# Four kinds of TensorE transposes replaced by DMAs in a four-layer graph kernel, sums by columns of ones, and pairs of graphs taking turns by a fixed row of steps

## The chip, the cores and the metric

The kernel runs on one core of a Trainium2 chip. The metric is the device time of one execution in microseconds (us), as the median of several executions. A single core has no neighbour to compare with, so an execution counts as slow only when it lies over 1.5% above the fastest of the same kernel.

## The reference, cut to what matters

64 graphs of 256 nodes with 256 features pass through four attention layers, each followed by a layer norm. Three places matter here: the softmax of layer 0 (its division by the sums), the broadcast sum `s1 + s2` of layer 2, and the adjacency matrix, which every layer uses as a mask.

```python
# layer 0: 4 heads of 64
attn = jnp.einsum('bhnd,bhmd->bhnm', q, k) * scale
attn = jax.nn.softmax(jnp.where(adj[:, None] == 0, NEG, attn), axis=-1)
out = jnp.einsum('bhnm,bhmd->bhnd', attn, v).transpose(...).reshape(Bx, Nx, C) @ Wo.T + bo
x = _layernorm(x + layer_norm(out) * gamma + beta)
# layer 1: 8 heads of 32, then y @ W1 -> gelu -> @ W2 + b2
...
# layer 2
Wh = h @ W;  s1 = Wh @ a1;  s2 = Wh @ a2
e = leaky_relu(s1[:, :, None] + s2[:, None, :], 0.2)
h_prime = softmax(where(adj > 0, e, NEG_INF), axis=2) @ Wh
# layer 3: scores (hidden * a0) @ hidden.T, leaky_relu, mask, softmax, @ hidden
```

## The kernel before

The kernel works on 32 pairs of graphs. A pair is a Python generator; each `yield` ends one step. Several pairs are under way at once, and the order in which their generators are advanced is, for the most part, the order in which the instructions stand in the engines' queues. Before, a new pair starts every 15 steps, and `rest` puts empty steps in.

The parts that the change touches (cuts marked with `...`; `matmul` and `transpose` are helpers, so nearly all TensorE instructions carry one of two line numbers, L567 and L570 before, L561 and L564 after):

```python
PACE = 15
REST = {"xn": 1, "e3": 2, "products 4": 1, "wh": 2, "mask": 2, "products 2": 1, "xT2": 1}
...
    def products(i, cs, v, es, hd, oT, sums, gamma=None):
        m = P // hd
        for n, c in enumerate(cs):
            po = ps_m.tile([P, 2, N], F32, name="pm")
            ...                                        # the products into po[:, 0, :]
            for kc in range(QB):                       # layer 0: sums, one row per head
                for h in range(m):
                    z = (2 * h + kc) * 32
                    matmul(po[z:z + 32, 1, :], pick[:, c, :], es[n][:, h, kc * N:(kc + 1) * N], start=True, stop=True)
            nc.scalar.copy(oT[:, c, :], po[:, 0, :])
            if c == 0:
                nc.scalar.copy(sums, po[:, 1, :])
            else:
                nc.vector.tensor_tensor(sums, sums, po[:, 1, :], ALU.add)
...
        def behind(i, oT, zs):                         # layer 0, after the products
            pz = sums_of(zs)                           # TensorE transposes of the sums
            r = r_0[:, g * G + i]
            nc.vector.tensor_reduce(r..., pz..., AX.X, ALU.add)
            nc.vector.reciprocal(r, r)
            rr = att.tile([P, QB, D], F32, name="rr")
            nc.vector.tensor_copy(rr..., r...to_broadcast([P, QB * 4, 64]))
            yield
            pr = ps_m.tile([P, NC, N], F32, name="pm")
            for c in range(NC):
                for q in range(QB):
                    transpose(pr[:, c, q * P:(q + 1) * P], rr[:, q, c * P:(c + 1) * P], ident)
            nc.vector.tensor_tensor(oT, oT, pr, ALU.mult)
            yield
            ...                                        # product with Wo ("WoT" in the traces)
...
        # layer 2: exp(s1) along every partition ("the row")
        ex = small.tile([P, TB, 3], F32, name="ex")
        nc.scalar.activation(ex, wh[:, :, D:D + 3], AF.Exp)
        pt = ps_m.tile([P, G, N], F32, name="pm")
        for t in range(TB):
            transpose(pt[:, t // QB, t % QB * P:(t % QB + 1) * P], ex[:, t, 0:1].to_broadcast([P, P]), ident)
        e = act.tile([P, G, QB, N], F32, name="qT")
        for t in range(TB):
            i, kc = divmod(t, QB)
            nc.vector.tensor_scalar(e[:, i, kc, :], pt[:, i, :], ex[:, t, 1:2], ex[:, t, 2:3], ALU.mult, ALU.max)
        nc.vector.tensor_tensor(e, e, mask, ALU.mult)  # views left out
...
        # at the start of a pair: the edges the other way round
        for t in range(TB):
            i, q = divmod(t, QB)
            for kc in range(QB):
                transpose(pt[:, i, kc, q * P:(q + 1) * P], adjb[:, t, kc * P:(kc + 1) * P], identb)
```

## Time and profile before

| | before |
|---|---|
| time | 2787.66 us (2786.94 to 2789.51) |
| TensorE busy | 2679.1 of 2784.8 us (96%) |
| VectorE, ScalarE, GpSimd busy | 69%, 47%, 21% |
| one pair of graphs | 83.77 us |
| TensorE idle per 84 us in the middle | 0.86 us |

A busy share near 100% says which engine sets the pace, but not what a microsecond taken from it is worth. For that one needs the repeated stretch: with 0.86 us idle in 84, every microsecond of TensorE's stream that goes away shortens a pair by as much, as long as no new wait takes its place, and every microsecond of a new wait lengthens it by as much. The prediction shows the lines.

### The profile page before, as it was taken

Reading aid. Unit: us, or ns where it says so; the run is one execution under the profiler, and the core shown is the slowest. Engines: PE = TensorE matmul, PEld = TensorE weight load, DVE = VectorE, ACT = ScalarE, POOL = GpSimd, SP = SyncE. Lnnn points to the kernel's source line nnn. Section 1 sums busy time; section 2 is a strip of 40 time slices with the busy share of each in tenths; the row PEclk is TensorE's granted clock in tenths of the full one; section 3 lists DMA queues with packets and bytes.
Section 4 is the critical chain, followed back from the end, with each engine's and each line's share of the span. In section 5 each row is a group of like instructions: output and inputs, shape, how many; then the busy total and the mean of one; then the engine's idle time right before and its main releaser. Section 6 shows DMA issues by size and latency. Waiting matters only on the chain.

```text
span 2784.8 us, 45617 instructions
## 1 busy us (share of the span) xinstructions
PE 2679.1 (96%) x17288; PEld 1842.6 (66%) x17288; DVE 1931.9 (69%) x6346; ACT 1295.8 (47%) x1953; POOL 578.4 (21%) x1138
## 2 busy tenths in 40 slices
PE   4899999999999999999999999999999999999996
PEld 2566666666667666667676667676666676666664
DVE  3666767776767776767776767777767777667764
ACT  2445445445444445444445444445444445444441
POOL 1112212212212212212212222212222212122211
PEclk9899999999999999999999999999999999999998
DMA  3000000000000000000000000000000000000000
GB/s 110 24 9 23 24 16 18 22 16 24 24 16 16 23 16 24 18 21 16 24 16 24 16 24 16 24 16 24 16 24 16 24 16 24 8 16 9 9 8 16
DMA packets 57905, 57.78 MB, mean 21 GB/s; under 512 B 5073, under 2 KB 57297, under 8 KB 57681
## 3 DMA queue, kind: packets, MB, share of 16 engines
q1 hardware_dynamic: 50784, 50.34, 5.9%
q10 hardware_dynamic: 6896, 4.47, 0.6%
q8 instruction: 139, 2.28, 0.3%
q14 instruction: 86, 0.70, 0.1%
HBM read 38.02 MB, written 16.78 MB: 20 GB/s over the span
## 4 chain that ended last, share of the span: by engine, by line
PE 68%; DVE 20%; POOL 8%; issue 2%; ACT 1%; DMA 1%; ACTq 0%; POOLq 0%; DVEq 0%
PE pm L567 53%; PE ps L567 9%; PE pm L570 6%; POOL rstd L590 6%; DVE xn L598 4%; DVE e L643 3%; DVE st L583 3%; POOL ve L586 2%; DVE z L598 1%; DVE mv L584 1%; DVE e L637 1%; ACT e L635 1%; DVE y L796 1%; DVE xb L802 1%; DVE xb L598 1%
## 5 line engine op out<-in xcount | busy, mean ns | idle before, releaser
L635 ACT ACTIVATE e<-ps 128x1024 f32<-128x1024 f32 x384 | 372.4, 1022 | 356.4 <-PE ps L567 353.3
L567 PE MATMUL pm<-L_gnn_W,hT 128*128 128x256 f32 x2048 | 463.2, 379 | 0.0
L567 PE MATMUL pm<-xT,L_gnn_W 128*128 128x512 f32 x1024 | 450.8, 593 | 0.0
L567 PEld LDWEIGHTS pm<-L_gnn_W,hT 128*128 128x128 f32 x2048 | 383.9, 190 | 63.2 <-issue 15.1
L643 DVE SCALAR_TENSOR_TENSOR e<-e,mask 128x256 f32<-128x256 f32 x1024 | 399.2, 453 | 29.2 <-ACT e L635 29.2
L840 ACT ACTIVATE hT<-pm,b 128x512 f32<-128x512 f32 x256 | 176.0, 688 | 477.8 <-PE pm L567 477.8
L586 POOL TENSOR_SCALAR ve<-mv 128x2 f32<-128x2 f32 x384 | 93.8, 244 | 1328.1 <-DVE mv L584 1131.9
L567 PEld LDWEIGHTS pm<-xT,L_gnn_W 128*128 128x128 f32 x1024 | 192.7, 191 | 216.6 <-issue 214.2
L590 POOL TENSOR_TENSOR rstd<-ve,mhalf 128x2 f32<-128x2 f32 (+1 forms) x384 | 298.4, 777 | 26.7
L583 DVE BATCH_NORM_STATS2 st<-y 128x6 f32<-128x256 f32 x768 | 299.8, 408 | 5.6
L598 DVE TENSOR_SCALAR xn<-y,mv,rstd 128x256 f32<-128x256 f32 x384 | 163.2, 471 | 127.6 <-POOL rstd L590 127.6
L923 DVE TENSOR_TENSOR qT<-qT,kT 128x1024 f32<-128x1024 f32 x32 | 39.2, 1225 | 195.2 <-ACT kT L922 195.2
L637 DVE TENSOR_TENSOR e<-e,mask 128x1024 f32<-128x1024 f32 x128 | 148.0, 1218 | 12.4 <-ACT e L635 12.4
L567 PE MATMUL pm<-e,z 128*32 128x256 f32 x2048 | 149.3, 385 | 3.5 <-DVE e L643 2.8
L567 PE MATMUL pm<-e,v 128*32 128x256 f32 x2048 | 135.5, 382 | 15.8 <-DVE e L637 15.8
L567 PE MATMUL ps<-xT 32*128 32x256 f32 x2048 | 148.0, 403 | 0.0
L826 POOL TENSOR_TENSOR both<-y,xb 128x512 f32<-128x512 f32 x64 | 81.7, 1276 | 313.2 <-DVE y L825 313.2
L764 POOL TENSOR_TENSOR x<-x,beta 128x1024 f32<-128x1024 f32 x32 | 75.7, 2365 | 324.7 <-PE pm L570 324.7
L616 ACT ACTIVATE xT<-pm,beta,gamma 128x512 f32<-128x512 f32 x128 | 92.9, 774 | 103.9 <-PE pm L570 103.6
L567 PE MATMUL ps<-qT,kT 64*128 64x256 f32 x1024 | 127.9, 389 | 0.6 <-ACT e L635 0.6
L567 PE MATMUL pm<-v,qT 128*128 128x260 f32 x512 | 120.3, 389 | 3.3 <-DVE qT L899 3.3
L567 PEld LDWEIGHTS ps<-xT 32*128 32x128 f32 x2048 | 93.3, 185 | 45.4 <-issue 42.1
(144 smaller groups left out, 4347.7 us busy)
## 6 DMA issues: line engine op xcount, KB each, us to landing
x<-in_x SPq DMA_DIRECT2D x32, 512.0 KB, 3.8
adj<-in_adj SPq DMA_DIRECT2D x32, 512.0 KB, 3.8
out<-xn SPq DMA_DIRECT2D x32, 512.0 KB, 2.9
L_gnn_W<-in_L_gnn_W ACTq DMA_DIRECT2D x2, 1024.0 KB, 7.3
L_gnn_WqT<-in_L_gnn_WqT ACTq DMA_DIRECT2D x1, 256.0 KB, 4.8
L_gnn_WkT<-in_L_gnn_WkT ACTq DMA_DIRECT2D x1, 256.0 KB, 6.7
L_gnn_WvT<-in_L_gnn_WvT ACTq DMA_DIRECT2D x1, 256.0 KB, 7.7
L_gnn_WoT<-in_L_gnn_WoT ACTq DMA_DIRECT2D x1, 256.0 KB, 8.9
```

The lines of the kernel that those rows point to most:

```text
L567: in_order(nc.tensor.matmul(*args, **kw))
L570: in_order(nc.tensor.transpose(*args))
L583: nc.vector.bn_stats(st[:, q, :], src[:, t, 0:D])
L586: nc.gpsimd.tensor_scalar(ve[:, 0], mv[:, :, 1], EPS, None, ALU.add)
L590: nc.gpsimd.tensor_tensor(rstd, ve, mhalf[:, 0:k * QB].rearrange("p (k t) -> p k t", k=k), ALU.pow)
L598: nc.vector.tensor_scalar(dst[:, t, 0:D], src[:, t, 0:D], mv[:, q, 0:1], rstd[:, q:q + 1], ALU.subtract, ALU.mult)
L616: nc.scalar.activation(dst[:, c, :], pt, AF.Identity, bias=bias[:, c:c + 1], scale=scale[:, c:c + 1])
L635: nc.scalar.activation(e, ps, AF.Exp, scale=scale)
L637: nc.vector.tensor_tensor(e, e, mask.unsqueeze(1).to_broadcast([P, 2, QB * N]), ALU.mult)
L643: nc.vector.scalar_tensor_tensor(e[:, h, k], e[:, h, k], 1.0, mask[:, k], ALU.mult, ALU.mult, accum_out=sums[:, kc, c, j:j + 1])
L826: nc.gpsimd.tensor_tensor(both[:, i * QB:(i + 1) * QB, 0:D], o, xi, ALU.add)
L840: nc.scalar.activation(hT[:, f, :], pm, AF.Gelu, bias=b1[:, f:f + 1])
```

## The change

The intent is to free TensorE of transposes. The edges are transposed by DMA. Layer 0's sums are taken by columns of ones, 32 equal rows a head; their reciprocals go to device memory and come back repeated over 64 partitions. Layer 2's row goes out element by element and comes back repeated over all partitions. The empty steps and the fixed pace give way to one row of digits, each the age of the pair that takes the next step.

```diff
-PACE = 15
-REST = {"xn": 1, "e3": 2, "products 4": 1, "wh": 2, "mask": 2, "products 2": 1, "xT2": 1}
+ORDER = "001122333421243112124212133210321220100201010"
...
+        pz = ps_m.tile([P, N], F32, name="pm")
+        for kc in range(QB):
+            for h in range(4):
+                matmul(pz[32 * h:32 * h + 32, :], ones[:, 0:32], es[h // 2][:, h % 2, kc * N:(kc + 1) * N], ...)
+        nc.scalar.copy(oT, po)
+        nc.vector.reciprocal(sums, pz)
+        nc.scalar.activation(pz, sums, AF.Copy, accum_out=tally[i])
...
-            pz = sums_of(zs)
-            ...
+            rr = att.tile([P, NC, N], F32, name="rr")
+            lines = dram.tile([NC, 2, N], F32, name="lines")
+            nc.sync.dma_start(lines.rearrange("c h n -> (c h) n"), rz[0:P:32, :])
+            for h in range(2):
+                nc.sync.dma_start(rr[h * 64:h * 64 + 64, :, :], lines[:, h, :].unsqueeze(0).to_broadcast([64, NC, N]))
...
-        for t in range(TB):
-            transpose(pt[:, t // QB, t % QB * P:(t % QB + 1) * P], ex[:, t, 0:1].to_broadcast([P, P]), ident)
+        line = dram.tile([T], F32, name="line")
+        nc.sync.dma_start(line.rearrange("(t p) -> p t", p=P), ex[:, :, 0])
+        row = att.tile([P, G, N], F32, name="row", bufs=1)
+        nc.sync.dma_start(row.rearrange("p g n -> p (g n)"), line.unsqueeze(0).to_broadcast([P, T]))
+        yield
...
-            for kc in range(QB):
-                transpose(pt[:, i, kc, q * P:(q + 1) * P], adjb[:, t, kc * P:(kc + 1) * P], identb)
+            nc.sync.dma_start_transpose(pt[:, i, :, q * P:(q + 1) * P], adjb[:, t, :])
...
-        if waiting and step % PACE == 0:
-            running.append(waiting.pop(0))
...
+        for age in ORDER:
+            g = period - int(age)
+            if 0 <= g < len(groups):
+                next(groups[g], END)
```

Besides, the bias row of W2's product is added by one instruction of 512 columns in place of two of 256.

More of the change, by code (lines that the diff above doesn't have):

```diff
@@ L411, in usual_input @@
     ps_m = ctx.enter_context(tc.tile_pool(name="ps_m", bufs=4, space=bass.MemoryType.PSUM))
+    dram = ctx.enter_context(tc.tile_pool(name="dram", bufs=2, space=bass.MemoryType.DRAM))
     ident = const.tile([P, P], F32, name="ident")
     make_identity(nc, ident)
-    identb = const.tile([P, P], BF16, name="identb")
-    nc.vector.tensor_copy(identb, ident)
     mhalf = const.tile([P, 2 * TB], F32, name="mhalf")
     nc.gpsimd.memset(mhalf, -0.5)
-    pick = const.tile([P, NC, 32], F32, name="pick")
-    nc.gpsimd.memset(pick, 0.0)
-    for c in range(NC):
-        nc.gpsimd.memset(pick[:, c, c:c + 1], 1.0)
     shift = const.tile([P, 1], F32, name="shift")
@@ L436, in usual_input @@
     edges = const.tile([P, B // G], F32, name="edges")
-    r_0 = const.tile([P, B, QB, 4], F32, name="r_0")
+    r_0 = const.tile([P, B], F32, name="r_0")
     r_3 = const.tile([P, B // G, TB], F32, name="r_3")
@@ L646, in scores, with products @@
         return es
-    def products(i, cs, v, es, hd, oT, sums, gamma=None):
+    def products(i, cs, v, es, hd, oT, sums, gamma, tally):
         m = P // hd
+        po = ps_m.tile([P, len(cs), N], F32, name="pm")
         for n, c in enumerate(cs):
-            po = ps_m.tile([P, 2, N], F32, name="pm")
             for kc in range(QB):
@@ L659, in products, with attention @@
                     e = es[n * (m // 2) + h // 2]
-                    matmul(po[r:r + 32, 0, :], v[:, i * QB + kc, c * P + r:c * P + r + 32],
+                    matmul(po[r:r + 32, n, :], v[:, i * QB + kc, c * P + r:c * P + r + 32],
                            e[:, h % 2, kc * N:(kc + 1) * N], start=kc == 0, stop=kc == QB - 1)
-            if gamma is not None:
-                nc.scalar.activation(oT[:, c, :], po[:, 0, :], AF.Identity, scale=gamma[:, c:c + 1])
-                continue
-            for kc in range(QB):
-                for h in range(m):
-                    z = (2 * h + kc) * 32
-                    matmul(po[z:z + 32, 1, :], pick[:, c, :], es[n][:, h, kc * N:(kc + 1) * N], start=True, stop=True)
-            nc.scalar.copy(oT[:, c, :], po[:, 0, :])
-            if c == 0:
-                nc.scalar.copy(sums, po[:, 1, :])
-            else:
-                nc.vector.tensor_tensor(sums, sums, po[:, 1, :], ALU.add)
-    def sums_of(zs):
-        pt = ps_m.tile([P, QB, P], F32, name="pm")
-        for q in range(QB):
-            transpose(pt[:, q, :], zs[:, q * P:(q + 1) * P], ident)
-        return pt
-    def rest(where):
-        for _ in range(REST.get(where, 0)):
-            yield
-    def attention(qT, kT, v, mask, hd, gamma, behind):
+        if gamma is not None:
+            nc.scalar.activation(oT[:, cs[0], :], po[:, 0, :], AF.Identity, scale=gamma[:, cs[0]:cs[0] + 1])
+            return
+        pz = ps_m.tile([P, N], F32, name="pm")
+        for kc in range(QB):
+            for h in range(4):
+                matmul(pz[32 * h:32 * h + 32, :], ones[:, 0:32], es[h // 2][:, h % 2, kc * N:(kc + 1) * N],
+                       start=kc == 0, stop=kc == QB - 1)
+        nc.scalar.copy(oT, po)
+        nc.vector.reciprocal(sums, pz)
+        nc.scalar.activation(pz, sums, AF.Copy, accum_out=tally[i])
+    def attention(qT, kT, v, mask, hd, gamma, behind, tally=None):
         scale = hd ** -0.5
@@ L713, in attention @@
                     after.append(behind(before[0], before[5], before[6]))
-                before = (i, cs, v, es, hd, oT, zs, gamma)
+                before = (i, cs, v, es, hd, oT, zs, gamma, tally)
                 yield
-                for _ in rest(f"scores {m}"):
-                    go_on()
-                    yield
         products(*before)
@@ L721, in attention @@
         yield
-        yield from rest(f"products {m}")
         while after:
@@ L732, in project @@
             pm = ps_m.tile([P, QB, D], F32, name="pm")
+            if row is not None:
+                matmul(pm, onesb, row.unsqueeze(1).to_broadcast([P, QB, D]), start=True, stop=False)
             for q in range(QB):
@@ L736, in project @@
                     matmul(pm[:, q, :], srcT[:, c, t * P:(t + 1) * P], w[:, c, :],
-                           start=c == 0, stop=c == chunks - 1 and row is None)
-                if row is not None:
-                    matmul(pm[:, q, :], onesb, row, start=False, stop=True)
+                           start=c == 0 and row is None, stop=c == chunks - 1 and (row is None or q == QB - 1))
                 if chunks > NC:
@@ L767, in layer0, with behind @@
         xb = act.tile([P, TB, D], F32, name="xb", tag="v")
-        def behind(i, oT, zs):
-            pz = sums_of(zs)
-            r = r_0[:, g * G + i]
-            nc.vector.tensor_reduce(r.rearrange("p q (c h) -> p q c h", c=NC),
-                                    pz.rearrange("p q (h k z) -> p q z h k", h=2, k=QB)[:, :, 0:NC], AX.X, ALU.add)
-            nc.vector.reciprocal(r, r)
-            rr = att.tile([P, QB, D], F32, name="rr")
-            nc.vector.tensor_copy(rr.rearrange("p q (h d) -> p (q h) d", d=64),
-                                  r.rearrange("p q h -> p (q h)").unsqueeze(2).to_broadcast([P, QB * 4, 64]))
-            yield
-            pr = ps_m.tile([P, NC, N], F32, name="pm")
-            for c in range(NC):
-                for q in range(QB):
-                    transpose(pr[:, c, q * P:(q + 1) * P], rr[:, q, c * P:(c + 1) * P], ident)
-            nc.vector.tensor_tensor(oT, oT, pr, ALU.mult)
+        def behind(i, oT, rz):
+            rr = att.tile([P, NC, N], F32, name="rr")
[3 more added lines that the diff above has]
+                nc.sync.dma_start(rr[h * 64:h * 64 + 64, :, :], lines[:, h, :].unsqueeze(0).to_broadcast([64, NC, N]))
+            yield
+            nc.vector.tensor_tensor(oT, oT, rr, ALU.mult)
             yield
@@ L803, in behind @@
             yield
-        yield from attention(qT, kT, v, mask, 64, None, behind)
+        yield from attention(qT, kT, v, mask, 64, None, behind, [r_0[:, g * G + i:g * G + i + 1] for i in range(G)])
         return xb, z
@@ L855, in renormed @@
         yield
-        yield from rest("xn")
         return xn
@@ L876, in layer2 @@
         yield
-        yield from rest("xT2")
         wh = act.tile([P, TB, W], F32, name="v")
@@ L886, in layer2 @@
         yield
-        yield from rest("wh")
         ex = small.tile([P, TB, 3], F32, name="ex")
         nc.scalar.activation(ex, wh[:, :, D:D + 3], AF.Exp)
-        pt = ps_m.tile([P, G, N], F32, name="pm")
-        for t in range(TB):
-            transpose(pt[:, t // QB, t % QB * P:(t % QB + 1) * P], ex[:, t, 0:1].to_broadcast([P, P]), ident)
+        line = dram.tile([T], F32, name="line")
[3 more added lines that the diff above has]
+        yield
         e = act.tile([P, G, QB, N], F32, name="qT")
@@ L897, in layer2 @@
             i, kc = divmod(t, QB)
-            nc.vector.tensor_scalar(e[:, i, kc, :], pt[:, i, :], ex[:, t, 1:2], ex[:, t, 2:3], ALU.mult, ALU.max)
+            nc.vector.tensor_scalar(e[:, i, kc, :], row[:, i, :], ex[:, t, 1:2], ex[:, t, 2:3], ALU.mult, ALU.max)
         nc.vector.tensor_tensor(e.rearrange("p g k q -> p (g k q)"), e.rearrange("p g k q -> p (g k q)"),
@@ L926, in layer3 @@
         yield
-        yield from rest("e3")
         return (yield from values_of(e, x, D, x, r_3[:, g], last[:, g]))
@@ L936, in group @@
         yield
-        pt = ps_m.tile([P, G, QB, N], BF16, name="pm")
+        pt = io.tile([P, G, QB, N], BF16, name="adjT", bufs=1)
         for t in range(TB):
             i, q = divmod(t, QB)
-            for kc in range(QB):
-                transpose(pt[:, i, kc, q * P:(q + 1) * P], adjb[:, t, kc * P:(kc + 1) * P], identb)
+            nc.sync.dma_start_transpose(pt[:, i, :, q * P:(q + 1) * P], adjb[:, t, :])
+        yield
         mask = act.tile([P, G, QB * N], BF16, name="mask")
@@ L947, in group @@
                                        accum_out=both_ways[:, g:g + 1])
-        yield from rest("mask")
         xb, z = yield from layer0(g, x, mask)
@@ L953, in group @@
         nc.sync.dma_start(out[g * G:(g + 1) * G].rearrange("b (q p) d -> p (b q) d", p=P), x[:, :, 0:D])
-    waiting = [group(g) for g in range(B // G)]
-    next(waiting[0])
-    running = []
-    step = 0
-    while waiting or running:
-        if waiting and step % PACE == 0:
-            running.append(waiting.pop(0))
-            if waiting:
-                next(waiting[0])
-        for r in list(running):
-            if next(r, END) == END:
-                running.remove(r)
-        step += 1
+    groups = [group(g) for g in range(B // G)]
+    next(groups[0])
+    for period in range(len(groups) + int(max(ORDER))):
+        if period + 1 < len(groups):
+            next(groups[period + 1])
+        for age in ORDER:
+            g = period - int(age)
+            if 0 <= g < len(groups):
+                next(groups[g], END)
+    assert all(next(g, END) == END for g in groups)
     good = const.tile([P, 7], F32, name="good")
     tops = const.tile([P, 7], F32, name="tops")
-    nc.vector.tensor_reduce(tops[:, 0:1], r_0.rearrange("p b q h -> p (b q h)"), AX.X, ALU.add)
+    nc.vector.tensor_reduce(tops[:, 0:1], r_0, AX.X, ALU.add)
     nc.vector.tensor_reduce(tops[:, 1:2], r_3.rearrange("p g t -> p (g t)"), AX.X, ALU.add)
```

## The prediction

> **What bounds the kernel now.** I read the page first (busy shares and slices), then the windows view by stretch of 84 us, then TensorE's timeline inside one repeated stretch.
>
> ```profile
> PE 2679.1 (96%) x17288; PEld 1842.6 (66%) x17288; DVE 1931.9 (69%) x6346; ACT 1295.8 (47%) x1953; POOL 578.4 (21%) x1138
> ...
> PE   4899999999999999999999999999999999999996
> ```
>
> TensorE is busy all through except in the first two slices and the last. The windows (columns: length, then busy us and instructions of PE, PEld, DVE, ACT, POOL, then granted clock, DMA share, GB/s) tell where its 105.7 idle us (2784.8 - 2679.1) lie:
>
> ```profile
> 0.00:84.00 84.00, 39.58 (x266) 26.02 (x266) 33.35 (x92) 23.71 (x37) 11.06 (x30) 0.90 0.35 104
> 84.00:168.00 84.00, 80.21 (x527) 49.16 (x520) 52.48 (x186) 40.38 (x57) 15.04 (x24) 0.98 0.05 13
> ...
> 1400.00:1484.00 84.00, 83.14 (x546) 57.27 (x544) 60.02 (x198) 40.43 (x61) 17.95 (x35) 1.00 0.06 20
> ...
> 2618.00:2702.00 84.00, 77.02 (x413) 53.60 (x412) 59.59 (x210) 32.88 (x48) 17.61 (x37) 0.98 0.02 7
> 2702.00:2785.00 83.00, 57.22 (x216) 41.84 (x214) 32.58 (x98) 16.81 (x26) 9.40 (x27) 0.85 0.04 14
> ```
>
> Fill: 44.4 + 3.8 = 48 us idle. Drain: 7.0 + 25.8 = 33 us. The middle: 0.86 us in each 84. The chain of waits repeats with a fixed period, which is one pair of graphs (32 pairs in all):
>
> ```profile
> 1239.41 8.47 PE pm L567 x41
> ...
> 1323.18 8.47 PE pm L567 x41
> ```
>
> 1323.18 - 1239.41 = 83.77 us a pair, 32 x 83.77 = 2681. So only two things count: TensorE time per pair (times 32), and the idle ends.
>
> [...]transposes of 279 ns mean occur every 0.11 us. So I count from one start to the next, never by duration. [...]The trace: 512 KB land in 3.8 us[...], 0.5 KB in 1.6.[...]
>
> **The change, part by part.** TensorE loses four kinds of transposes. Starts within one period (start, us, engine, line, what):
>
> ```profile
> 1446.80 0.60 PE L570 MATMUL pm<-ident,zs 128*128 128x128 f32 x4
> 1447.23 1.04 PE L570 MATMUL pm<-ident,xb 128*128 128x128 f32 x8
> 1448.33 1.07 PE L570 MATMUL pm<-ident,rr 128*128 128x128 f32 x8
> 1449.23 0.60 PE L570 MATMUL pm<-ident,ex 128*128 128x128 f32 x4
> 1449.66 3.60 PE L567 MATMUL pm<-xT,L_gnn_W 128*128 128x512 f32 x8
> ...
> 1470.36 0.61 PE L570 MATMUL pm<-identb,adjb 128*128 128x128 bf16 x8
> 1470.81 1.04 PE L570 MATMUL pm<-ident,xn 128*128 128x128 f32 x8
> ```
>
> zs 1447.23 - 1446.80 = 0.43, rr 0.90, ex 0.43, adjb 0.45: together 2.21 us a pair. All lie in the stream that sets the end.
>
> ```profile
> 1399.95 0.27 PE L567 MATMUL pm<-b2m,onesb 128*128 128x256 bf16 x1
> 1400.15 1.15 PE L567 MATMUL ps<-xT 32*128 32x256 f32 x16
> ...
> 1437.15 1.07 PE L567 MATMUL pm<-e,v 128*32 128x256 f32 x16 [0.55 <-DVE e L637]
> ```
>
> The bias row costs 0.20 each, four a pair: 0.8. It becomes two of 512 columns; I estimate 0.3 each, so 0.2 is saved. The sums by "pick" (eight instructions, 0.43 us, four times a pair) become sums by ones, with the same number of 32-column matmuls: 0. Total: 2.4 us a pair, x 32 = 77 us, or 2.8%. The 0.55 us wait for the mask product looks the same in the new order (scores, 1 us of other work, scores, products), so I leave it.
>
> VectorE: it loses the zs additions (26.7 us), the rr copies (24.2), the reduction (11.2) and its small reciprocal (10.4), 72.5 in all. It gains 64 reciprocals of 256 columns, whose price follows from two rows:
>
> ```profile
> L816 DVE RECIPROCAL r<-r 128x16 f32<-128x16 f32 x64 | 15.8, 247 | 1.1
> L774 DVE RECIPROCAL r<-r 128x8 f32<-128x8 f32 x64 | 10.4, 198 | 0.1
> ```
>
> (247 - 198) / 8 = 6.1 ns per column, so 256 take 198 + 248 x 6.1 = 1.7 us (estimate), x 64 = 109 us. VectorE ends near 1931.9 - 72.5 + 109 = 1968 us of some 2710 (73%): not the bound. ScalarE: 64 copies of 512 instead of 128 + 64 of 256, and 64 activations with a sum: about even. The built order keeps one Gelu and one Exp table load per pair.
>
> The DMAs take the place of work that TensorE did in order, so each result now comes later. With u = 0 where graph 0's products end, from the built order: wh 3.6, layer 3's values 3.5, yT 1, WoT 3.45, W1 3.45, then layer 2's values.
> - 1/sums: reciprocal 1.7, write some 2, read some 2.5: graph 0 is laid out at about u = 6.3, graph 1 at 9.7. WoT starts at u = 11.2. Hidden, some 3 us to spare.
> - Layer 2's row: its Exp is ready at u = 7.3; the write of 512 single elements some 3.5 to 4 us, the read 3: on hand at u = 14 to 14.5. Then four products of 0.47 (L898), an eviction 0.69 and the mask 1.2: done at 17.5 to 18.2. Layer 2's values want it at u = 18.1. At the edge: 0 to 0.5 us of stall.
> - Edges: counted from the end of layer 3's scores, adjb is done at 3.5, four transposes at about 7.5 (estimate: 0.5 issue each, 2 to land), the mask at 8.7. VectorE waits some 3 us for it, then has 4.3 us of layer 1's mask products (8 x 0.53) which TensorE wants at 13.9. About 0.9 us to spare.
>
> The ends: the row of steps has ages 0 to 4, so four thin periods instead of three lanes 15 steps apart. By my count of ages 0, 1, 2, 3, 4, TensorE's work is 20.7, 14, 30, 11.5 and 3.6 us. At the start one pair alone goes through layer 0 with the round trips exposed (some 4 us more than the 3.2 us its transposes took), and at the end the row's round trip stands open once or twice (7 us each). I put 10 us on fill and drain together (a judgement, 0 to 25), and take back 8 us of the 0.86 us idle per period, as a hand-made row should be laid to avoid waits. Sum: 2787.7 - 77 + 10 - 8 = 2713; as the row was presumably chosen by measured time, I lean a little lower: 2710.
>
> **The rivals.** (a) A DMA wait takes the place of the transposes. For: the two slim margins above, VectorE's strict queue, in which a wait for the row or the mask also holds back evictions, and one queue (SP) that issues 14 DMAs a pair and sits through each round trip. Against: TensorE's 64 to 70 us of other work per pair, and DMA share 0.06. If each of two chains is 1 us late, 2 x 32 = 64 us come back: some 2770. (b) Buffers: the sum's PSUM tile is now held until reciprocal and ScalarE are through (u = 5.9 for graph 1), and the fourth tile of wh wants it at u = 5.8. If VectorE is 1 us behind, 32 us come back: some 2740. (c) The transposes were cheap anyway because they filled gaps (their start-to-start overstates them): against it, TensorE had no gaps there. It would give 2740 to 2760. (d) The row also removes the 0.86 us a period and shortens the ends: 2680.
>
> **Range and chances.** The 77 us are firm, the rest is waits. 2% faster means under 2732, which leaves 22 us over my number, or 0.7 us of new stall per pair; two margins are about that thin, so a quarter to a third of the weight lies beyond it. Slower by 2% needs over 4 us of stall per pair, hardly. Range 2668 to 2765.
>
> **What would show it.** Right: a period near 81.3 us, TensorE busy 2600 or so, the four transpose rows gone, reciprocal near 1.7 us, VectorE waiting on DMA for the row and the mask but TensorE hardly on VectorE. Wrong: TensorE rows with idle behind the mask or layer 2's products of 1 us or more per pair, transposing DMAs over 5 us from issue to landing, or thin ends longer by over 25 us.

## The result, and the profile after

The changed kernel takes 3026.42 us (3025.66 to 3027.53, four runs), the kernel before on the same chip 2788.59 us (four runs). The ratio is 1.0854, with a 95% interval of 1.0835 to 1.0873: 8.5% slower. Here and below a ratio is the mean time of one kernel's fast runs over that of the other's of the same rounds, so it is not quite the ratio of the medians quoted beside it.

The page of the kernel before has these lines on DMA packets and on the chain of waits that ended last (its shares by engine):

```profile
DMA packets 57905, 57.78 MB, mean 21 GB/s; under 512 B 5073, under 2 KB 57297, under 8 KB 57681
...
PE 68%; DVE 20%; POOL 8%; issue 2%; ACT 1%; DMA 1%; ACTq 0%; POOLq 0%; DVEq 0%
```

The page of the changed kernel answers with the following (busy times, packets, chain):

```profile
PE 2689.2 (89%) x16456; PEld 1816.3 (60%) x16456; DVE 1966.1 (65%) x6153; ACT 1285.9 (43%) x1953; POOL 576.7 (19%) x1135
...
DMA packets 135212, 91.61 MB, mean 30 GB/s; under 512 B 61648, under 2 KB 130512, under 8 KB 134992
...
PE 67%; DMA 15%; DVE 10%; POOL 4%; ACT 1%; issue 1%; SPq 1%; ACTq 0%; DVEq 0%; POOLq 0%
```

TensorE has 832 instructions fewer (17288 to 16456) and is yet busy 10 us longer, in a span that is 239 us longer: its idle time rose from 105.7 to 3023.6 - 2689.2 = 334.4 us. DMA, 1% of the old chain, holds 15% of the new one. The packets (the pieces into which the page divides a transfer) below 512 bytes grew from 5,073 to 61,648. Three questions follow: what does TensorE wait for, why is it busy longer with less work, and which of the three new kinds of DMA is to blame.

The view of waits of the changed kernel (engine, tile and line that waited, what ended the wait; then us in all, times, longest) answers the first:

```profile
DVE oT L754 <- DMA rr<-lines: 193.5, 32, 8.3
...
PE pm L561 <- DVE oT L754: 169.9, 31, 7.7
...
DVE qT L867 <- DMA row<-line: 100.7, 32, 8.8
...
PE pm L561 <- DVE r L838: 51.6, 25, 2.7
...
PE pm L561 <- DVE qT L868: 15.4, 7, 14.0
```

Read upwards in pairs: TensorE's product with Wo waits for VectorE's `oT * rr` (169.9 us), which waits for the DMA that repeats the reciprocals (193.5 us), once in each of the 32 pairs. The direct wait for the row, which the prediction had at the edge, costs TensorE only 15.4 us.

One such wait in TensorE's timeline of the changed kernel (start, us, what, count, in brackets the idle time before and what ended it):

```profile
1476.64 1.89 PE L561 MATMUL pm<-L_gnn_WoT,oT 128*128 128x256 f32 x8
1486.05 3.75 PE L561 MATMUL pm<-L_gnn_WoT,oT 128*128 128x256 f32 x8 [7.51 <-DVE oT L754]
1489.59 4.52 PE L561 MATMUL pm<-xT,L_gnn_W 128*128 128x512 f32 x8
```

Graph 0's eight products take 1.89 us; graph 1's come after 7.51 us of idling and take 3.75, twice as long for the same eight instructions. The eight of W1 behind them take 4.52 us, where the prediction's fence shows 3.60 before. This is the answer to the second question, and the window of one period shows the same in its granted clock, the share of full speed that the throttle allows TensorE (the column after the five busy times):

```profile
1405.73:1496.00 90.27, 82.76 (x508) 55.74 (x509) 60.07 (x189) 40.06 (x61) 17.85 (x35) 0.92 0.11 28
```

The clock was 1.00 in the middle of the kernel before. The trace shows a mean of 0.92 in this window, and doubled durations right behind a 7.51 us wait (3.75 us in place of 1.89). How long a wait it takes for the clock to fall, or how much work for it to rise again, was not shown. The groups of instructions show the sum of it for the product with Wo, first before, then after (busy us, mean ns of one, then idle before it):

```profile
L567 PE MATMUL pm<-L_gnn_WoT,oT 128*128 128x256 f32 x512 | 115.8, 379 | 0.0
```

```profile
L561 PE MATMUL pm<-L_gnn_WoT,oT 128*128 128x256 f32 x512 | 177.4, 508 | 179.4 <-DVE oT L754 169.9 <-DVE mv L578 9.6
```

The same 512 instructions: 379 ns each before with no idle time, 508 ns after with 179.4 us of it. The new reciprocal has this row among VectorE's groups of the changed kernel:

```profile
L665 DVE RECIPROCAL zs<-pm 128x256 f32<-128x256 f32 x64 | 112.0, 1750 | 7.3 <-PE pm L561 6.8
```

Its 1750 ns are the predicted price, so the arithmetic that came new isn't the trouble.

Why does the read of the reciprocals take so long? Its issues on the queue of SP (SyncE, which issues these DMAs) in that period, from SP's timeline of the changed kernel:

```profile
1441.77 5.27 SPq L910 DMA_TRANSPOSE adjT<-adjb  x4
...
1473.15 0.37 SPq L860 DMA_DIRECT2D line<-ex  x1
1473.61 1.24 SPq L752 DMA_DIRECT2D rr<-lines  x2
1483.74 0.34 SPq L862 DMA_DIRECT2D row<-line  x1
```

Just before graph 1's read (1473.61) stands the write of layer 2's row, 512 single elements (1473.15). The read of the row, which must wait for that write, is issued at 1483.74, 10.6 us later. The chain of waits in two periods (start, us, what) has either the one or the other:

```profile
1474.25 10.84 DMA rr<-lines
...
1563.15 8.96 DMA line<-ex
...
1572.13 4.77 DMA row<-line
```

The period grew from 83.77 to 90.47 us ((1586.67 - 1405.73) / 2, between starts of W1's second quarter two pairs apart). So the suspicion is that the element-wise write is slow, and that graph 1's reciprocals stand in line behind it. Whether they do, and what the other parts of the change are worth, the trace of one kernel can't tell.

### The profile page after: what moved, and what is told of

Same layout as the page of the kernel before. It is cut to its first block, busy times and chain, and to the rows that moved or that the text cites.

```text
span 3023.6 us, 44337 instructions
## 1 busy us (share of the span) xinstructions
PE 2689.2 (89%) x16456; PEld 1816.3 (60%) x16456; DVE 1966.1 (65%) x6153; ACT 1285.9 (43%) x1953; POOL 576.7 (19%) x1135
## 2 busy tenths in 40 slices
DMA packets 135212, 91.61 MB, mean 30 GB/s; under 512 B 61648, under 2 KB 130512, under 8 KB 134992
## 4 chain that ended last, share of the span: by engine, by line
PE 67%; DMA 15%; DVE 10%; POOL 4%; ACT 1%; issue 1%; SPq 1%; ACTq 0%; DVEq 0%; POOLq 0%
PE pm L561 50%; PE ps L561 12%; DMA line<-ex 9%; PE pm L564 5%; DMA row<-line 4%; POOL rstd L584 3%; DVE qT L867 1%; DVE st L577 1%; DMA rr<-lines 1%; DVE y L766 1%; DVE y L761 1%; DVE qT L868 1%; DVE xn L592 1%; POOL ve L580 1%; DVE y L839 1%
## 5 line engine op out<-in xcount | busy, mean ns | idle before, releaser
L561 PE MATMUL pm<-xT,L_gnn_W 128*128 128x512 f32 x1024 | 489.1, 634 | 51.6 <-DVE r L838 51.6
L637 DVE SCALAR_TENSOR_TENSOR e<-e,mask 128x256 f32<-128x256 f32 x1024 | 364.0, 419 | 154.6 <-ACT e L629 154.5
L561 PEld LDWEIGHTS pm<-xT,L_gnn_W 128*128 128x128 f32 x1024 | 210.5, 208 | 303.9 <-issue 288.6
L561 PE MATMUL pm<-L_gnn_WoT,oT 128*128 128x256 f32 x512 | 177.4, 508 | 179.4 <-DVE oT L754 169.9
L592 DVE TENSOR_SCALAR xn<-y,mv,rstd 128x256 f32<-128x256 f32 x384 | 206.2, 572 | 163.4 <-POOL rstd L584 163.4
L561 PEld LDWEIGHTS pm<-L_gnn_WoT,oT 128*128 128x128 f32 x512 | 125.8, 258 | 214.3 <-issue 185.3
L754 DVE TENSOR_TENSOR oT<-oT,rr 128x512 f32<-128x512 f32 x64 | 44.1, 689 | 193.5 <-DMA rr<-lines 193.5
L610 ACT ACTIVATE xT<-pm,beta,gamma 128x512 f32<-128x512 f32 x128 | 92.7, 773 | 126.8 <-PE pm L564 126.4
L561 PE MATMUL pm<-v,qT 128*128 128x260 f32 x512 | 122.3, 393 | 23.2 <-DVE qT L868 15.4
L561 PE MATMUL pm<-e,z 128*32 128x256 f32 x2048 | 140.0, 387 | 0.1
L561 PEld LDWEIGHTS pm<-v,qT 128*128 128x128 f32 x512 | 99.3, 196 | 55.5 <-issue 31.4
```

The source lines that it names most:

```text
L561: in_order(nc.tensor.matmul(*args, **kw))
L592: nc.vector.tensor_scalar(dst[:, t, 0:D], src[:, t, 0:D], mv[:, q, 0:1], rstd[:, q:q + 1], ALU.subtract, ALU.mult)
L610: nc.scalar.activation(dst[:, c, :], pt, AF.Identity, bias=bias[:, c:c + 1], scale=scale[:, c:c + 1])
L637: nc.vector.scalar_tensor_tensor(e[:, h, k], e[:, h, k], 1.0, mask[:, k], ALU.mult, ALU.mult, accum_out=sums[:, kc, c, j:j + 1])
```

## The experiments

Twelve kernels ran, all with correct results, each beside the kernel before on the same chip.

### The write of single elements

**The row back on TensorE.** Everything else stays as in the changed kernel.

```diff
-        nc.sync.dma_start(line.rearrange("(t p) -> p t", p=P), ex[:, :, 0])
-        nc.sync.dma_start(row.rearrange("p g n -> p (g n)"), line.unsqueeze(0).to_broadcast([P, T]))
+        pt = ps_m.tile([P, G, N], F32, name="pm")
+        for t in range(TB):
+            transpose(pt[:, t // QB, t % QB * P:(t % QB + 1) * P], ex[:, t, 0:1].to_broadcast([P, P]), ident)
```

> Layer 2's row goes back to TensorE (four transposes of ex into PSUM, right after wh); the write of 512 single elements and the read of the row are gone, everything else stays as changed, the row of steps too. My theory (the element-wise write, some 9 us long, makes both waits: 1/sums of graph 1 queued behind it, and the row itself late): both waits vanish, the wait of WoT for oT falls from 5.6 us a pair to under 0.5, the period falls from 90.5 us to 82 to 83 (81.3, plus 0.43 for the transposes, plus up to 1 us in which TensorE waits for ex), the clock is back at 0.98 or more, total 2735 to 2770. Rival 'the row of steps is to blame': the period stays over 87, total over 2900. Rival 'the round trip of 1/sums is to blame by itself': WoT still waits 4 us or more, total over 2880.

Measured: 2825.47 us (2823.24 to 2828.79), ratio 1.0139 (1.0122 to 1.0156), mean granted clock 0.987 against 0.946. The wait before Wo's product fell from 169.9 to 6.8 us, as the theory said, and 201 us came back:

```profile
PE pm L561 <- DVE oT L754: 6.8, 2, 5.4
```

But the time expected, 2735 to 2770, was missed. The trace has small waits in place of the large one, per pair 0.71 us for the Exp in front of the transposes, 0.95 for an eviction (VectorE emptying a tile of PSUM, into which TensorE writes its results), 0.43 for ScalarE's `xT` and 1.45 before W1's second quarter.

**The same, with the write issued but never read.** If the cause is the row's lateness, an unread write costs nothing; if the write holds up others, it costs nearly all.

```diff
         line = dram.tile([T], F32, name="line")
         nc.sync.dma_start(line.rearrange("(t p) -> p t", p=P), ex[:, :, 0])      # nobody reads it
+        ... the row by TensorE, as above
```

> As the run with the row back on TensorE (2825), but the element-wise write of ex is still issued, at its old place in SP's queue, and nobody reads it. My theory (the write [...]delays the reads of graph 1's 1/sums whoever needs it): WoT waits for oT 4 us or more a pair again, the clock falls to about 0.95, period 88 to 91, total 2930 to 3040. Rival 'only the lateness of the row counts': no such wait, total within 1% of 2825.

Measured: 3055.51 us (3053.8 to 3056.19), ratio 1.0964, clock 0.946. The write alone, which nothing waits for, costs 230 us over the run without it. Its view of waits, then its chain of waits:

```profile
DVE oT L754 <- DMA rr<-lines: 194.0, 32, 8.2
```

```profile
1402.78 10.69 DMA rr<-lines
```

VectorE's wait for graph 1's reciprocals is the same 194 us as in the changed kernel. This shows the delay apart from the row's own lateness: the 2 KB write holds up a read that has nothing to do with it, for 10.69 us in the period above. It even costs more than in the changed kernel, because here the evictions of layer 3's values stand behind `oT * rr` in VectorE's queue, and TensorE's next transposes (of `xb`) wait for those, 213.6 us in all.

**The write in runs of 16 bytes.** The elements of one partition are kept together, so 128 runs of four elements go out; the reader takes the row in the other order.

```diff
-        ex = small.tile([P, TB, 3], F32, name="ex")
-        nc.sync.dma_start(line.rearrange("(t p) -> p t", p=P), ex[:, :, 0])
+        ex = small.tile([P, 3, TB], F32, name="ex")
+        nc.sync.dma_start(line.rearrange("(p t) -> p t", t=TB), ex[:, 0, :])
...
-            nc.vector.tensor_scalar(e[:, i, kc, :], row[:, i, :], ...)
+            nc.vector.tensor_scalar(e[:, i, kc, :]..., row[:, :, i * QB:(i + 1) * QB].rearrange("p q t -> p t q"), ...)
```

> The row is kept in the order partition-major: the write is 128 runs of 16 bytes instead of 512 elements of 4 bytes, the read is as before, and the products read the row with a stride of 4 elements. If the write's time goes by the number of its pieces, it falls from 9 us to some 3.5 us, 1/sums of graph 1 comes in time, the row is on hand 5.5 us earlier, and layer 2's values wait some 1 us: period 82 to 83.5, total 2740 to 2790. If its time does not go by the pieces but is the latency of small writes to memory: total within 2% of 3026.

Measured: 2755.87 us (2755.18 to 2757.14), ratio 0.9889 (0.9873 to 0.9906). One access pattern is worth 270 us, and the kernel with it is 1.1% faster than before. Its chain of waits, then TensorE's timeline:

```profile
1438.11 2.54 DMA line<-ex
1440.66 3.52 DMA row<-line
```

```profile
1454.36 10.54 PE L561 MATMUL pm<-xT,L_gnn_W 128*128 128x512 f32 x24 [2.20 <-DVE r L838]
```

The same 2 KB go out in 2.54 us in place of 8.96. The page's packet count falls by 135,212 - 122,924 = 12,288, which is 32 pairs times 384, exactly the 512 elements less 128 runs. TensorE is busy 2603.4 us, and the clock is back at 0.986. So of the 270.5 us between the two profiled spans (3023.6 - 2753.1), 2689.2 - 2603.4 = 85.8 are TensorE's busy time, longer at the slower clock (0.946 against 0.986), and 184.7 are idle time, 172.5 of which are the two waits named above (169.9 + 15.4, against 6.8 + 6.0 here). The runs don't separate the number of the packets from their size, which changed with it. What is left in front of W1's second quarter, 48.0 us in all, was there in the changed kernel too (51.6) and is taken up further below:

```profile
PE pm L561 <- DVE r L838: 48.0, 30, 2.4
```

**The write from ScalarE's queue.** If the queue of SP is what makes the read wait, another queue frees it.

```diff
-        nc.sync.dma_start(line.rearrange("(t p) -> p t", p=P), ex[:, :, 0])
+        nc.scalar.dma_start(line.rearrange("(t p) -> p t", p=P), ex[:, :, 0])
```

> Only the element-wise write is issued from ScalarE's queue; the rest as changed. If queueing of the reads of 1/sums behind the write within SP's queue is a mechanism of its own, WoT no longer waits (under 1 us a pair), but the row comes as late as before (Exp to row some 14 us), so layer 2's values now wait 5 to 6 us: period 86 to 89, total 2880 to 2990. Rival 'queueing is all of it': period near 82, total under 2780. Rival '[...]the issuing queue is of no account': WoT still waits 5 us or more, total within 1% of the changed kernel, 3000 to 3050.

Measured: 2973.6 us (2967.39 to 2978.05), ratio 1.0662, clock 0.948. The time lies inside the range of my theory, 2880 to 2990, but by luck: the wait before Wo's product was to fall under 1 us a pair, and layer 2's values were to wait 5 to 6 us a pair, while TensorE's wait for their products came to 19.3 us in all. The line that decides:

```profile
PE pm L561 <- DVE oT L754: 126.8, 30, 5.7
```

The wait falls from 169.9 to 126.8 us only, so the queue of issue has a part in it, 43.1 us, but the smaller one: 4 us a pair are left. By what the write from another queue still holds up the read was not shown. The write itself took 9.25 us from the other queue. Here the long list of tiny packets had to be made shorter; moving it was not enough.

### The new row of steps

**The row of steps alone**, with all the old parts.

```diff
-PACE = 15  ...  rest(...)
+ORDER = "001122333421243112124212133210321220100201010"
```

> The kernel before with the new row of steps alone: all transposes on TensorE, sums by pick, no new DMA (two empty steps keep the row in step). My theory: the row of steps does no harm by itself: period 83 to 85 us (83.8 less or plus a microsecond for transposes that follow their source at once), total 2770 to 2830. Rival 'the row of steps is to blame': period over 87, total over 2900.

Measured: 2945.05 us (2944.42 to 2948.07), ratio 1.0566 at an undisturbed clock of 0.987. I had expected 2770 to 2830. With the old parts the new row does harm: six new waits stand in each pair, 2.03 for the sums, 0.69 for the reciprocals, 0.71 for the Exp, 0.34, 0.43 and 1.46, together 5.7 us, and the period is 88.79. The two that belong to the old way of repeating 1/sums:

```profile
PE pm L571 <- DVE zs L674: 63.6, 32, 2.0
...
PE pm L571 <- DVE r L775: 21.4, 31, 0.7
```

**The new parts (with 16-byte runs) and the old turns**, every 15 steps.

```diff
-    for period in range(len(groups) + int(max(ORDER))): ...
+    ... if waiting and step % PACE == 0: running.append(waiting.pop(0)) ...
```

> The new parts with the 16-byte write, but with the groups' turns of the kernel before (three lanes 15 steps apart with its rests, two of which are one shorter because the new parts bring a step each). My theory: the new parts need the new row of steps (their round trips want 8 to 10 us between source and use, the old turns leave 8 to 9), as the new row needs the new parts: TensorE waits 2 to 5 us a pair for oT or for layer 2's products, total 2790 to 2900. Rival 'the turns are of no account': within 1% of 2756. Rival 'the old turns are the better ones': under 2728.

Measured: 2865.67 us (2864.28 to 2868.95), ratio 1.0287, inside the expected range. The waits fit less well: TensorE waits 42.8 us in all, 1.4 a pair, for layer 2's products and 5.5 us once for oT, where 2 to 5 us a pair were expected. Of the 110 us between the two spans (2863.1 and 2753.1), 44.5 are idle time and 65.5 busy time, with the same 16456 instructions and the same clock, 0.986. About half of the busy time, 34 us, lies at layer 1's products (174.0 us against 139.9 with the 16-byte runs). In the period looked at, one of the four groups of 16 products takes 2.23 us and the others 1.07. Over the whole kernel VectorE's mask products for them take 483 ns each in place of 420, and GpSimd's `x + beta` takes 3.27 us against 2.37 in the kernel before. No run tests what joins these, and the other half stays open.

With these two runs the square is complete:

| | old turns | new row of steps |
|---|---|---|
| old parts | 2787 us | 2945 us |
| new parts, 16-byte runs | 2866 us | 2756 us |

Either half alone is slower than neither, and both together are faster. So the parts and the turns belong together; a sum of separate gains, which is how the prediction was built, has no place for that.

**Layer 0's sums and 1/sums as before**, with the new row of steps and the 16-byte runs.

```diff
-        pz = ... ones ...;  nc.vector.reciprocal(sums, pz)
-            lines = dram.tile(...);  two reads into rr
+        ... pick, sums_of(zs), tensor_reduce, small reciprocal, tensor_copy, eight transposes, as in the kernel before
```

> The kernel with the row written in 16-byte runs, with layer 0's sums taken by single columns and their reciprocals repeated by TensorE as in the kernel before. My theory (the row of steps is laid for results that come without TensorE's round trips, so each old part brings its own wait back): 42 us of transposes (1.33 us a pair) and some 2.7 us a pair of waits at zs and rr: 2830 to 2900 us. Rival (the transposes are all that the change saves here): 2756 + 42 = 2798 us, within 1%.

Measured: 2941.08 us (2933.19 to 2949.49), ratio 1.055: 185 us over the run with DMA, more than I had expected. Its spans and busy times divide it: idle time rose by 232.7 - 149.7 = 83 us, for which the two old waits stand with the very totals that the row of steps alone had (63.6 and 21.4; the wait before W1's second quarter, 58.9 us, is near the 48.0 of before), and busy time by 2708.5 - 2603.4 = 105 us, where the transposes explain 42 (1.33 a pair in the prediction's fence). The other 63 come with a lower clock, 0.964 against 0.986, behind waits of only 2 us:

```profile
1436.18 0.60 PE L568 MATMUL pm<-ident,zs 128*128 128x128 f32 x2 [2.03 <-DVE zs L671]
1437.47 1.94 PE L568 MATMUL pm<-ident,rr 128*128 128x128 f32 x8 [0.69 <-DVE r L763]
1439.21 5.62 PE L565 MATMUL pm<-wx,xT 128*128 128x259 f32 x16
```

The 16 products of the last line take 3.77 us with the 16-byte runs. The run with the row of steps alone has the same two waits and hardly a drop (these products take 404 ns each there, 453 here, 391 with the 16-byte runs); what tells these two cases apart stays open. With this run it is shown that layer 0's 1/sums by DMA are the part on which the new row of steps leans most: undone alone, they cost 185 us, 63 of them with the lower clock. The first run above gives the same measure for layer 2's row, 2825.47 - 2755.87 = 70 us, and the next one gives it for the edges, 13 us. The three don't add up to the 189 us that undoing all of them costs (2945.05 - 2755.87).

### The edges

**Edges by TensorE again**, the rest as with the 16-byte runs.

```diff
-            nc.sync.dma_start_transpose(pt[:, i, :, q * P:(q + 1) * P], adjb[:, t, :])
+            for kc in range(QB):
+                transpose(pt[:, i, kc, q * P:(q + 1) * P], adjb[:, t, kc * P:(kc + 1) * P], identb)
```

> The 16-byte write, and the edges transposed on TensorE again (eight bf16 transposes a pair, 0.45 us from start to start before). If the DMA transposes are hidden and free: 32 x 0.45 = 14 us more than 2756, so 2765 to 2780. Rival 'they cost as much as they save' (they hold SP's queue 5 us a pair, and the mask waited on them): 2745 to 2760.

Measured: 2768.45 us (2765.59 to 2771.22), ratio 0.9939. The difference to the 16-byte runs, 12.6 us or 0.39 us a pair, is near the 0.45 us that the four transposing DMAs take off TensorE's stream. In the changed kernel they hold SP for 5.27 us a pair, and no wait of TensorE is put down to them.

### The 1.5 us that stayed before W1's second quarter

The run with 16-byte runs waits there for VectorE, which empties tiles of layer 2's values. In VectorE's queue, layer 0's scaling stands ahead of that.

**Layer 2's values one quarter later**, by two exchanged digits in the row.

```diff
-ORDER = "001122333421243112124212133210321220100201010"
+ORDER = "001122333421241123124212133210321220100201010"
```

> The 16-byte write, and one step of the row moved: layer 2's values after the second quarter of W1 instead of before it. In the 16-byte run TensorE waits 2.2 us in a pair (48 us in all) before that quarter for VectorE, which has not emptied the PSUM tiles of layer 2's values (its queue is full of layer 0's statistics then). If it is that backlog, the wait falls under 0.5 us, period 80.8 to 81.5, total 2700 to 2730. Rival 'VectorE is behind all the time': the wait only moves to the next quarter, total within 0.5% of 2756.

Measured: 2954.82 us (2951.69 to 2955.41), ratio 1.0605. A miss: the row fixes TensorE's order, but not VectorE's, and in this trace the evictions have moved behind layer 0's statistics. TensorE waits 179.4 us for them (31 times), and the clock is 0.955.

**VectorE's order forced**: the evictions go before layer 0's scaling; the row of steps stays.

```diff
+                tc.add_manual_dep(ins.ins, emptied[0], ...)    # ins: layer 0's scaling; emptied: the last eviction of layer 2's values
```

> The kernel with the row written in 16-byte runs (2755.9 us) still waits 1.5 us a pair (48 us in all) in front of the second quarter of W1, for VectorE emptying a tile of layer 2's values: in VectorE's queue layer 0's scaling stands ahead of it. Here one order is forced: the emptying of layer 2's values goes before layer 0's scaling; the row of steps stays. My theory (the wait is VectorE's queue order): the wait before W1 goes nearly whole, but layer 0's output is now ready later, so its transposes may wait 1.5 to 3 us: 2720 to 2790 us. Rival (the wait is VectorE's total backlog, whatever its order): the wait only moves and the time stays within 0.5% of 2756.

Measured: 2753.6 us (2753.24 to 2754.17), ratio 0.9879 (0.9863 to 0.9896). The wait before W1 fell from 48.0 to 14.9 us, and one of 30.9 us came up before layer 0's transposes. The wait has moved, as the rival said. The 2.3 us less in all are within the noise of the two intervals, and the time fits theory and rival alike; the waits decide.

**The same, with layer 0's transposes one step later.**

```diff
-ORDER = "001122333421243112124212133210321220100201010"
+ORDER = "001122333421243112124221332103121220100201010"
```

> As the run before it, and in the row of steps layer 0's transposes (zT) come one step later, behind the first product with W2, so that the scaling has time. My theory: both waits gone, 1.5 us a pair, 48 us, less some 10 for new small ones: 2700 to 2735 us. Rival (VectorE's backlog only moves): a wait of 1 us or more a pair stands in front of another product, and the time is 2750 or above.

Measured: 2885.18 us (2882.85 to 2903.81), ratio 1.0349. The wait before layer 0's transposes is gone, but moving one step moved others: new waits of 0.18 and 1.38 us before the transposes of layer 2's output and 1.58 before layer 1's scores, for ScalarE to empty layer 3's. The clock was 0.973 in the profiled run, the slowest of the five, and 0.979 to 0.981 in the others. The rival's "2750 or above" holds, my theory's number doesn't.

**Less work for VectorE there**: half of layer 2's mask product goes to GpSimd, with the forced order.

```diff
-        nc.vector.tensor_tensor(e, e, mask, ALU.mult)          # both graphs
+        for i in range(G):
+            (nc.vector if i == 0 else nc.gpsimd).tensor_tensor(e[:, i], e[:, i], mask[:, i], ALU.mult)
```

> The run with 16-byte runs and the forced order (2753.6 us) showed that the wait of 1.5 us a pair had only been split: 0.7 us before W1's second quarter and 0.95 us before layer 0's transposes, as VectorE's backlog behind the row predicts. Here VectorE's backlog is made smaller: of layer 2's mask product (128x1024, 1.22 us on VectorE) graph 1's half goes to GpSimd, whose 128x512 product takes 1.26 us in the trace and which is idle then. Theory (backlog): VectorE has 0.6 us less to do there, so each of the two waits falls by 0.6 us, 1.0 to 1.2 us a pair, 32 to 38 us: 2712 to 2730 us. Rival (GpSimd's half comes late for layer 2's products, or delays the statistics that follow on GpSimd by as much): a new wait of 0.5 to 1 us a pair takes the gain back, 2740 to 2765 us.

Measured: 2747.12 us (2744.97 to 2747.83), ratio 0.9857 (0.984 to 0.9873). This is the fastest kernel of all that ran, but its interval touches those of the 16-byte runs (0.9873 to 0.9906) and of the forced order (0.9863 to 0.9896), and the theory behind it fell: VectorE had 0.6 us less to do, and both waits stayed, 0.69 us and 0.96 us in the period looked at. Over the whole kernel the one before W1 fell from 14.9 to 9.1 us, and the one before layer 0's transposes stayed, 31.1 us against 30.9. TensorE's timeline of it, then VectorE's:

```profile
1446.75 10.54 PE L561 MATMUL pm<-xT,L_gnn_W 128*128 128x512 f32 x24 [0.69 <-DVE r L844]
```

```profile
1444.29 0.73 DVE L594 TENSOR_SCALAR xn<-y,mv,rstd 128x256 f32<-128x256 f32 x2 [0.85 <-POOL rstd L586]
```

VectorE isn't backlogged here; it stands idle for 0.85 us, waiting for GpSimd's `rstd`, less than 2 us before the eviction that TensorE wants. Before layer 0's transposes it waits 1.39 us in the same way. So the remaining wait looks like round trips of statistics between VectorE and GpSimd in front of the evictions. That is read from the trace and was not tested by a run.

## Why the prediction was wrong, by its own steps

**TensorE's saving of 77 us: right.** With the clock back, TensorE is busy 2603.4 us against 2679.1, 75.7 less; the predicted row was "2600 or so". The edges' share, 0.45 us a pair or 14.4 us, measured 12.6.

**The reciprocal and VectorE's total: right.** 1750 ns measured for an estimate of 1.7 us, and 1966.1 us in all for 1968. That the total fits to 2 us is luck: layer 1's mask products fell from 399.2 to 364.0 us and the scaling of `xn` rose from 163.2 to 206.2, neither of which was foreseen. VectorE isn't the bound.

**The edges: right in the result, not in the reckoning.** The mask waited for the transposes three times in the kernel, 12.9 us in all, and no wait of TensorE is put down to it. But the margin was not 0.9 us, nor did VectorE wait 3 us a pair: in the period looked at the mask starts at 1439.32, before the next pair's transposes are issued at 1441.77, so these have most of a period to land. An issue took 1.3 us (5.27 / 4) and not the 0.5 of the estimate; SP's plain issues took 0.37 to 0.61 us in the first 32 us of the kernel before.

**The row: the step that failed.** It reads "the write of 512 single elements some 3.5 to 4 us, the read 3", and concludes "0 to 0.5 us of stall". Both times were estimates, which no run had shown: the write took 8.96 us in one period and 10.6 from its issue to the next issue in another, the read 4.77. With 128 runs they took 2.54 and 3.52, which would have fitted the step. The row's own lateness cost TensorE little directly (15.4 us); the larger loss came by the next step.

**1/sums "hidden, some 3 us to spare": right alone, wrong in company, and with 169.9 us of wait the costliest error.** Each chain was worked out as though no other transfer were under way. Graph 1's read is issued 0.46 us after the row's write and took 10.84 us in place of 2.5, the estimate (in the kernel before, 0.5 KB took 1.6 us and 512 KB 3.8). Behind the write of 128 runs, graph 1's read, issued at 1438.54, is multiplied in at 1442.41, 3.9 us later, with a wait of 0.40; the 3 us to spare are then enough. The dummy write shows that this delay, not the row's own lateness, carries the loss.

**The clock: not in the prediction at all.** It had no term for work that stays the same and takes longer. TensorE was busy 85.8 us longer with the same instructions, about a third of the 270 us.

**The ends, "10 us": near.** With the 16-byte runs the first and the last 168 us hold 62.1 + 35.2 = 97.3 us of idle time, against 48 + 33 = 81 before: 16 us, within the 0 to 25 allowed.

**"Take back 8 us" of the idle time per period: wrong in sign.** Even the kernel without the slow write idles 82.43 - 80.16 = 2.27 us in the period looked at, and its idle time between the ends is 149.7 - 97.3 = 52.4 us, against 105.7 - 81 = 24.7 before: 28 us more in place of 8 less. The prediction asked whether each new transfer would be in time, but not what the new row of steps does to waits that have no transfer in them. Of the 46 us between 2710 and the 2755.9 us of the kernel with 16-byte runs, which lies inside the range of 2668 to 2765, this is 36; the ends are 6, the lean to a lower number 3.

The rivals: (a) had the right place, "a DMA wait takes the place of the transposes", and reckoned with 1 us a chain where 5.5 to 7.5 came. (b), PSUM tiles emptied too late by VectorE, is the kind of wait that the 48 us are, only of other tiles than it named. (c) falls with the 75.7 us, and (d) with the waits of the new row. SP issues 15 DMAs a pair, not the 14 of rival (a), which changes nothing. That "slower by 2%" was given hardly a chance came from taking a stall of over 4 us a pair as hardly possible, which holds only while each wait is looked at alone.

## What to carry to other kernels

Count a DMA's packets before its bytes: here 2 KB as 512 elements took three and a half times as long as in 128 runs (8.96 us against 2.54), and the transfer issued shortly after it paid as well (10.84 us), for the larger part even with the write on another queue (126.8 of 169.9 us of wait). When a margin of a few microseconds hides a transfer, list all transfers that are under way in the same stretch and ask what the largest packet count among them does to the margin. And where a kernel's turns have been laid by hand to fit its parts, test the parts and the turns in all four combinations; here neither had a value of its own.
